# Attention scores kept in their banks: later key tiles add products with differences of neighbouring keys

## The chip, the core and the metric

The kernel runs on one core of a Trainium2 chip. The core has five engines that run at the same time and wait for each other through semaphores: TensorE (PE in the profile; PEld is its loading of weights), VectorE (DVE), ScalarE (ACT), GpSimd (POOL) and SyncE (SP), which issues most of the DMAs. Matrix products land in PSUM, in banks of 512 float32 columns per partition; DVE and ACT can read PSUM, POOL works on SBUF alone. The metric is the device time of one execution in microseconds (us).

## What is computed

The block of the reference is a gated transformer block over `x` of 8 x 1024 x 512, with a context of 8 x 1024 x 384. All of it is float32:

```
x = x + tanh(g1) * cross_attention(layernorm(x), ctx)        # 8 heads of 64
x = x + tanh(g2) * ffn(layernorm(x))                         # 16 heads of 32

cross_attention: q = x Wq, k = ctx Wk, v = ctx Wv; softmax(q k^T / 8) v; then Wo, bo
ffn:  q, k, v = x W^T + b
      q = (q / |q| + query_embedding) * softplus(temperature)
      h = softmax(q k^T / sqrt(32)) v
      out = (h * sum of gates) Wp^T + bp      # gates: top 3 of 15 routed heads and a shared one
```

What the change touches is the middle of both attentions: the scores `q k^T` less the row maximum, which the exponential is taken of.

## The kernel before

The batch is taken element by element (8 of them). Each has four chunks of kind 1 (cross attention, two heads of 64 in 128 partitions) and four of kind 2 (the second attention, four heads of 32). A chunk of either kind does the following.

- **Projections.** `project` computes `q` and `k` of the chunk, transposed: 128 rows (heads by width) x 1024 positions, in two halves of 512. Kind 2 also normalises q (`project_q`, `norms`, `scaled_q`): ACT writes `qq`, POOL squares it into `rn` (L367), PE sums the squares by head (`pn`), ACT takes logarithm and exponential (L391, L392), POOL multiplies (L393), ACT scales (L400).
- **Maxima.** POOL makes bfloat16 copies `kb` and `qb` (L409). PE multiplies them (`pm`, L424) and DVE takes the maximum over the keys (L465, or L448 with two banks at a time). The 16 or 32 rows of negated maxima go through a transpose (`pr`) and four small DMAs (L480) into the rows of `sh`: for every query of every head, minus a maximum of its scores.
- **Scores.** `attention` goes through steps (h, s): h is the half of the queries (512 of them), s the key tile. A step of kind 1 has two key tiles of 128 for two heads, so there are 4 steps in a half; a step of kind 2 has one key tile for four heads, so 8. In `score` two tiles of two banks each are taken from the pool `ps_sc`, which has exactly two such tiles, and each of the four banks gets two products: a one-row product of `ones_b` with a row of `sh`, which puts minus the maximum into every key's row (`m == 0`, `start=True`), and then the product of 128 keys with 512 queries (`m == 1`). ACT takes the exponential of each tile (L522) into `e`. In kind 2 each half of a step (tile 0 or 1) is written in turn, and which half comes first is switched when a pair of maxima products stood just before (`taken`), so that it begins with partitions that those did not use.
- **Values and sums.** `value` multiplies `e` with `v` into `av` (L609). POOL adds pairs of `e` tiles (L527), DVE adds some of these to a running one (L540), and the remaining ones are summed over the keys on PE with `ones` (`summed`, L560). ACT turns the sum into its inverse (L584, L585) and POOL multiplies (L596).

The order of the work on PE, ACT, DVE and POOL is written out by the program itself: the schedule is manual, and instructions stand in each engine's queue in the order in which the Python code emits them. A small planner keeps modelled clocks (`at["PE"]`, `at["DVE"]`, `at["POOL"]`). Constants such as `SC` (the cost of a step's scores) move these clocks, and they decide when a filler (a projection or an output product), a pair of maxima products, or a deferred action from the lists `soon` and `later` is emitted; `add` leaves a sum of exponentials to DVE only when its modelled clock is near PE's, and otherwise hands one more tile to the sums on PE. Between the two attentions `between` computes the output of kind 1, the second layernorm, and the first projections of kind 2; there, `project_q` of the second chunk first empties the list `soon`, which holds the first chunk's `scaled_q`, its copy into `kb` and `begin_maxima`, with the copy into `qb`.

Tiles come from pools by name: `k` has three buffers, `rn` one, the exponentials nine, the general PSUM tiles three.

Of the kernel before, what the change touches and what calls it, by code (L numbers as in the profile page):

```python
# [10 lines left out]
F32 = mybir.dt.float32  # L11
BF16 = mybir.dt.bfloat16
AF = mybir.ActivationFunctionType
ALU = mybir.AluOpType
AX = mybir.AxisListType

P = 128
# [4 lines left out]
def tile_gated_block(  # L22
# [38 lines left out]
    nc = tc.nc  # L61
# [5 lines left out]
    H = 512  # L67
# [13 lines left out]
    work = ctx.enter_context(tc.tile_pool(name="work", bufs=2))  # L81
# [3 lines left out]
    ps_sc = ctx.enter_context(tc.tile_pool(name="ps_sc", bufs=2, space=bass.MemoryType.PSUM))  # L85
# [120 lines left out]
    def norm(xt, key):  # L206

        mv = small.tile([P, 2], F32, tag="mv", name=f"mv_{key}", bufs=2)
        rs = small.tile([P, 1], F32, tag="rs", name=f"rs_{key}", bufs=2)
        xn = work.tile([P, D], F32, tag="wa", name=f"xn_{key}", bufs=4)  # L210
        stats(mv, xt, key)
        inverse(rs, mv)
        scaled(xn, xt, mv)
        return xn
# [41 lines left out]
    at = {"PE": 0.0, "DVE": 0.0, "POOL": 0.0}  # L256
# [10 lines left out]
    def pe(ns):  # L267
        at["PE"] += ns
# [4 lines left out]
    def pool(ns):  # L273
        at["POOL"] = max(at["POOL"], at["PE"]) + ns
# [21 lines left out]
    class Chunk:  # L296


        def __init__(self, kind, b, c):
            self.kind, self.b, self.c = kind, b, c  # L300
            self.key = f"{kind}_{b}_{c}"
            self.width = HD1 if kind == 1 else HD2
            self.nh = P // self.width
            self.nk = 4 // self.nh
            self.ns = NT // self.nk
            self.mx, self.done, self.free, self.waiting = None, 0, 0.0, False

            self.ends = (kind, b, c) == (2, B - 1, ND - 1)
            self.SC = 2200 if kind == 1 else 1250
            self.steps = [(h, s) for h in range(NH) for s in range(self.ns)]  # L310

        def loads(self, what="kq"):
# [18 lines left out]
        def project(self, st):  # L331

            begun = self.waiting
            if not begun:
                self.placed()
            halves = range(NH)
            if self.kind == 1:
                for h in halves:
                    yield from self.project_k(st, h)
                soon.append((at["PE"] + 3000, self.copied, self.kb, self.k))  # L340
                for h in halves:
                    yield from self.project_q(st, h)
            else:
                for h in halves:
                    yield from self.project_q(st, h)
                    if h or not begun:
                        yield from self.project_k(st, h)
                    yield from self.norms(h)
                soon.append((at["PE"] + 1000, self.copied, self.kb, self.k))
            soon.append((at["PE"] + 3000, self.begin_maxima))  # L350

        def project_q(self, st, h):
# [55 lines left out]
        def copied(self, out, src):  # L408
            nc.gpsimd.tensor_copy(out, src)  # L409
            pool(1050)  # L410

        def begin_maxima(self):
            self.copied(self.qb, self.q)
            self.waiting = False
            self.mx, self.done, self.free = self.maxima(), 0, at["POOL"] + 1500
# [73 lines left out]
        def score(self, step):  # L489

            h, s = step
            nh, width, key = self.nh, self.width, self.key
            order = (1, 0) if taken[0] and self.kind == 2 else (0, 1)
            taken[0] = False
            pss = {
                u: ps_sc.tile([P, 2, H], F32, tag="sc", name=f"sc_{key}_{h}_{s}_{u}") for u in order
            }

            def products(m, u):
                for j in (2 * u, 2 * u + 1):
                    kk, i = divmod(j, nh)
                    r, kc = i * width, s * self.nk + kk
                    if m == 0:
                        r += kk * HD2
                        lhsT, rhs = ones_b[r : r + 1, :], self.sh[r : r + 1, ts(h, H)]
                    else:
                        rows = slice(r, r + width)
                        lhsT, rhs = self.k[rows, ts(kc, P)], self.q[rows, ts(h, H)]  # L510
                    nc.tensor.matmul(pss[u][:, j % 2, :], lhsT=lhsT, rhs=rhs, start=(m == 0), stop=(m == 1))  # L511


            for half in [order] if self.kind == 1 else [order[:1], order[1:]]:
                for m in range(2):
                    for u in half:
                        products(m, u)
            pe(self.SC)
            e = {}
            for u in order:  # L520
                e[u] = epool.tile([P, 2, H], F32, tag="e", name=f"e_{key}_{h}_{s}_{u}")
                nc.scalar.activation(e[u], pss[u], AF.Exp)  # L522
            self.e[step] = e
# [141 lines left out]
    later, soon = [], []  # L665
# [430 lines left out]
    for t in range(NT):  # L1096
        was, xn = xn, norm(st.x[t], f"1_0_{t}")
# [91 lines left out]
```

## Time and profile before

| what | value |
|---|---|
| runs | 4901.2, 4903.87 and 4914.34 us; median 4903.87 |
| profiled execution | span 4892.8 us, from its first to its last instruction |
| around the span | the median of the runs lies 11.1 us above it; the profiled execution's own device time isn't listed apart |
| clock granted to TensorE | 0.991 of full speed on average |
| PE, DVE, ACT, POOL busy | 97%, 63%, 46%, 52% of the span |
| one element of the batch | about 605 us: 210 of kind 1, 128 between, 267 of kind 2 |

How to read the lines that follow: a group has the source line, the engine, the operation, what it writes and reads by the program's names, the shape, how often, then busy time and the mean ns of one, then how long the engine stood idle before these instructions and who ended that. In a timeline each line is a run of equal instructions: start, length, engine, line, operation, count. PE records are modelled at their ends and overlap, so what an instruction costs in a dense stretch is the distance from its start to the next start. An fp32 product has two records on PE and a bfloat16 product one.

### The profile page before, as it was taken

Reading aid. Unit: us, or ns where it says so; the run is one execution under the profiler, and the core shown is the slowest. Engines: PE = TensorE matmul, PEld = TensorE weight load, DVE = VectorE, ACT = ScalarE, POOL = GpSimd, SP = SyncE. Lnnn points to the kernel's source line nnn. Section 1 sums busy time; section 2 is a strip of 40 time slices with the busy share of each in tenths; the row PEclk is TensorE's granted clock in tenths of the full one; section 3 lists DMA queues with packets and bytes.
Section 4 is the critical chain, followed back from the end, with each engine's and each line's share of the span. In section 5 each row is a group of like instructions: output and inputs, shape, how many; then the busy total and the mean of one; then the engine's idle time right before and its main releaser. Section 6 shows DMA issues by size and latency. Waiting matters only on the chain.

```text
span 4892.8 us, 83962 instructions
## 1 busy us (share of the span) xinstructions
PE 4741.9 (97%) x35196; PEld 1428.3 (29%) x35196; DVE 3104.2 (63%) x4225; ACT 2254.3 (46%) x2916; POOL 2566.8 (52%) x1346
## 2 busy tenths in 40 slices
PE   9999999999999999999999999999999999999998
PEld 2222232222322223222232222322223222232232
DVE  4557665576656765567655576556765567655674
ACT  3435634355343553435534365343552436524364
POOL 1636646366363663636636366363663636626474
PEclk9999999999999999999999999999999999999999
DMA  2020010200103001030010300202002020010100
GB/s 81 27 97 20 26 50 27 97 22 24 50 27 102 17 24 50 27 106 14 24 57 24 102 14 24 65 23 95 14 24 68 27 88 15 16 53 25 38 1 18
DMA packets 212682, 208.11 MB, mean 43 GB/s; under 512 B 24144, under 2 KB 147024, under 8 KB 212304
## 3 DMA queue, kind: packets, MB, share of 16 engines
q1 hardware_dynamic: 212016, 202.76, 13.0%
q8 instruction: 275, 4.51, 0.4%
q14 instruction: 103, 0.84, 0.1%
q10 hardware_dynamic: 288, 0.00, 0.0%
HBM read 153.93 MB, written 48.23 MB: 41 GB/s over the span
## 4 chain that ended last, share of the span: by engine, by line
PE 78%; DVE 12%; POOL 3%; issue 3%; ACT 2%; DMA 1%; SPq 1%; ACTq 0%; DVEq 0%; POOLq 0%
PE sc L511 20%; PE av L609 17%; PE po L282 9%; PE pq L282 8%; PE pm L424 7%; PE pk L282 7%; PE pv L282 5%; DVE mx L448 4%; DVE mx L465 4%; PE sum L560 4%; DVE e L540 3%; POOL e L527 2%; ACT e L522 1%; PE pn L282 1%; SPq L480 1%
## 5 line engine op out<-in xcount | busy, mean ns | idle before, releaser
L527 POOL TENSOR_TENSOR e<-e,e 128x1024 f32<-128x1024 f32 x764 | 1858.8, 2448 | 1127.2 <-PE av L609 640.9
L522 ACT ACTIVATE e<-sc 128x1024 f32<-128x1024 f32 x1536 | 1492.6, 1021 | 1228.4 <-PE sc L511 1194.1
L465 DVE TENSOR_REDUCE mx<-pm 128x1 f32<-128x512 f32 x2332 | 1485.7, 684 | 751.9 <-PE pm L424 707.7
L511 PE MATMUL sc<-q,k 32*128 32x512 f32 (+1 forms) x6144 | 1197.8, 607 | 0.0
L609 PE MATMUL av<-e,v 128*32 128x512 f32 (+1 forms) x6144 | 1082.8, 614 | 0.0
L540 DVE TENSOR_TENSOR e<-e,e 128x1024 f32<-128x1024 f32 x427 | 803.8, 1893 | 347.6 <-POOL e L527 346.6
L424 PE MATMUL pm<-kb,qb 32*128 32x512 bf16 (+1 forms) x3072 | 630.7, 384 | 61.4 <-DVE mx L465 29.8
L448 DVE TENSOR_REDUCE mx<-pm 128x2 f32<-128x1024 f32 x370 | 427.7, 1218 | 264.8 <-PE pm L424 264.8
L511 PEld LDWEIGHTS sc<-q,k 32*128 32x128 f32 (+1 forms) x6144 | 479.3, 190 | 205.4 <-issue 192.1
L511 PE MATMUL sc<-sh,ones_b 1*128 1x512 bf16 x3072 | 412.6, 386 | 32.2 <-ACT e L522 16.1
L424 PEld LDWEIGHTS <-qb 32*128 32x128 bf16 (+1 forms) x3072 | 153.2, 92 | 931.6 <-issue 921.6
L609 PEld LDWEIGHTS av<-e,v 128*32 128x32 f32 (+1 forms) x6144 | 194.4, 118 | 617.3 <-issue 600.8
L282 PE MATMUL pq<-y1T,wq 128*32 128x512 f32 (+1 forms) x1568 | 249.6, 600 | 6.5 <-ACT r L584 2.6
L282 PE MATMUL pq<-y2T,wq 128*32 128x512 f32 x2048 | 248.6, 606 | 2.8 <-ACT rn L391 2.8
L282 PE MATMUL pk<-y2T,wk 128*32 128x512 f32 x2048 | 243.3, 595 | 0.0
L282 PE MATMUL pv<-wv,y2T 128*32 128x512 f32 x2048 | 242.8, 597 | 0.0
L282 PE MATMUL po<-wp,h2T 128*64 128x512 f32 (+1 forms) x1152 | 231.1, 596 | 0.0
L282 PE MATMUL po<-wo,h1T 128*32 128x512 f32 x2048 | 223.1, 593 | 0.0
L511 PEld LDWEIGHTS <-ones_b 1*128 1x128 bf16 x3072 | 103.3, 91 | 385.0 <-issue 360.9
L560 PE MATMUL sum<-e,ones 128*32 128x512 f32 (+1 forms) x1380 | 209.8, 595 | 0.2 <-POOL e L527 0.2
L282 PE MATMUL pk<-ctx,wk 128*32 128x512 f32 (+1 forms) x1176 | 188.7, 603 | 19.5 <-DMA ctx<-in_ctx 5.9
L393 POOL TENSOR_TENSOR qq<-qq,rn 128x512 f32<-128x512 f32 x64 | 89.6, 1400 | 207.6 <-ACT rn L392 200.0
(110 smaller groups left out, 2777.6 us busy)
## 6 DMA issues: line engine op xcount, KB each, us to landing
y<-xn SPq DMA_DIRECT2D x120, 256.0 KB
xb<-y SPq DMA_DIRECT2D x480, 64.0 KB
x<-in_x SPq DMA_DIRECT2D x64, 256.0 KB
out<-x SPq DMA_DIRECT2D x64, 256.0 KB
xs<-in_x SPq DMA_DIRECT2D x56, 256.0 KB
xn<-in_x SPq DMA_DIRECT2D x56, 256.0 KB
ctx<-in_ctx SPq DMA_DIRECT2D x7, 1536.0 KB
wq<-in_L_xattn_Wq SPq DMA_DIRECT2D x32, 256.0 KB
```

Source lines behind the costliest of these rows:

```text
L282: nc.tensor.matmul(ps[ts(j, w), :], lhsT=lhsT[:, ts(j, w)], rhs=rhs, start=start, stop=stop)
L393: nc.gpsimd.tensor_tensor(self.qq, self.qq, rn, ALU.mult)
L424: nc.tensor.matmul(ps, lhsT=self.qb[ts(i, width), ts(c, P)], rhs=self.kb[ts(i, width), ts(kh, H)], start=True, stop=True,)
L448: nc.vector.tensor_reduce(out, tiles[u], AX.X, ALU.max)
L465: nc.vector.tensor_reduce(mx[:, i * NT + c, kh : kh + 1], ps, AX.X, ALU.max)
L480: nc.sync.dma_start(out=self.sh[r : r + 1, :].rearrange("o (c q) -> o c q", c=NT), in_=rows[ts(r // width, NT), :],)
L511: nc.tensor.matmul(pss[u][:, j % 2, :], lhsT=lhsT, rhs=rhs, start=(m == 0), stop=(m == 1))
L522: nc.scalar.activation(e[u], pss[u], AF.Exp)
L527: nc.gpsimd.tensor_tensor(one, one, two, ALU.add)
L540: nc.vector.tensor_tensor(accs[-1], accs[-1], a, ALU.add)
L560: nc.tensor.matmul(ps[ts(2 * u + j, self.width), :], lhsT=ones[:, 0 : self.width], rhs=acc[n][:, j, :], start=(n == 0), stop=(n == len(acc ...
L609: nc.tensor.matmul(self.av[ts(i, width), :], lhsT=st.v[:, kc, ts(self.c * self.nh + i, width)], rhs=e[j // 2][:, j % 2, :], start=(kc == 0 ...
```

## The change

The two score tiles are taken once per half of the queries, at its first step, and kept for all its steps. The one-row products with `sh` are made at the first step only. Their sum with the first key tile's product stays in the banks, and every later step adds, without `start`, the product of the queries with the difference between this key tile and the one before in the same bank. ACT reads the banks after each step, as before.

For this the keys are turned into differences in place, after their bfloat16 copy is made: `differences` runs once per chunk. ACT copies the odd steps' keys into `was` (a buffer of the tag `rn`), POOL subtracts the even steps' keys from the odd ones, and then the copied odd ones from the even ones that follow. With w the columns of a step, these are 512 columns for the copy and the first subtraction and 256 (kind 1) or 384 (kind 2) for the second. It is put into `soon` behind the copy into `kb`, before `begin_maxima` with the copy into `qb`. The planner's cost of a step's scores is lowered from 2200 to 1950 ns and from 1250 to 1050 ns, and POOL's modelled clock is moved by 2500 ns for the differences.

Since a tile belongs to half u for a whole half of the queries, the switch of the order in kind 2 no longer decides which buffer is written first: before, the half that came first got the buffer next in turn.

```diff
-            self.SC = 2200 if kind == 1 else 1250
+            self.SC = 1950 if kind == 1 else 1050
...
                 soon.append((at["PE"] + 3000, self.copied, self.kb, self.k))
+                soon.append((at["PE"] + 3000, self.differences))
...
                 soon.append((at["PE"] + 1000, self.copied, self.kb, self.k))
+                soon.append((at["PE"] + 1000, self.differences))
             soon.append((at["PE"] + 3000, self.begin_maxima))
...
+        def differences(self):
+
+            w, n = self.nk * P, self.ns // 2
+            even, odd = (
+                self.k.rearrange("p (s o w) -> p o s w", o=2, w=w)[:, o] for o in range(2)
+            )
+            was = work.tile([P, n, w], F32, tag="rn", name=f"was_{self.key}", bufs=1)
+            nc.scalar.copy(was, odd)
+            nc.gpsimd.tensor_tensor(odd, odd, even, ALU.subtract)
+            nc.gpsimd.tensor_tensor(
+                even[:, 1:n], even[:, 1:n], was[:, 0 : n - 1], ALU.subtract
+            )
+            pool(2500)
...
-            pss = {
-                u: ps_sc.tile([P, 2, H], F32, tag="sc", name=f"sc_{key}_{h}_{s}_{u}") for u in order
-            }
+            if s == 0:
+                self.pss = {
+                    u: ps_sc.tile([P, 2, H], F32, tag="sc", name=f"sc_{key}_{h}_{u}") for u in order
+                }
+            pss = self.pss
...
-                    nc.tensor.matmul(pss[u][:, j % 2, :], lhsT=lhsT, rhs=rhs, start=(m == 0), stop=(m == 1))
+                    nc.tensor.matmul(pss[u][:, j % 2, :], lhsT=lhsT, rhs=rhs, start=(m == 0), stop=(m == 1), skip_group_check=True)
...
-                for m in range(2):
+                for m in range(1 if s else 0, 2):
```

## The prediction

> **What bounds the kernel now.** I read the page first: busy time by engine, then the chain of work that ended last.
>
> ```profile
> PE 4741.9 (97%) x35196; PEld 1428.3 (29%) x35196; DVE 3104.2 (63%) x4225; ACT 2254.3 (46%) x2916; POOL 2566.8 (52%) x1346
> ...
> PE 78%; DVE 12%; POOL 3%; issue 3%; ACT 2%; DMA 1%; SPq 1%; ACTq 0%; DVEq 0%; POOLq 0%
> ```
>
> TensorE (PE) has work 97% of the time and carries 78% of the chain. One fifth of the chain runs over other engines, so the stages have to be looked at apart. Busy time by stage of batch 3: FFN-type attention, cross attention, and the stretch between the two (columns: stretch; time; PE, weight loads, DVE, ACT, POOL busy; clock; DMA share; GB/s):
>
> ```profile
> 1595.80:1862.30 266.50, 257.31 (x2160) 77.52 (x2158) 197.61 (x244) 155.96 (x185) 179.09 (x82) 0.99 0.06 18
> 1862.30:2072.00 209.70, 208.12 (x1119) 65.41 (x1119) 116.66 (x195) 79.42 (x102) 100.00 (x51) 1.00 0.14 43
> 2072.00:2200.40 128.40, 123.03 (x1078) 34.33 (x1074) 75.93 (x90) 45.02 (x76) 43.30 (x36) 1.00 0.31 101
> ```
>
> Kind 1 (second row) is PE and nothing else. Kind 2 (first row) has PE at 97% with DVE at 74% and POOL at 67%: there other engines can be last. Next the groups that the change touches, different shapes apart:
>
> ```profile
> L522 ACT ACTIVATE e<-sc 128x1024 f32<-128x1024 f32 x1536 | 1492.6, 1021 | 1228.4 <-PE sc L511 1194.1 <-DVE e L540 29.6 <-PE pm L424 1.8
> ...
> L540 DVE TENSOR_TENSOR e<-e,e 128x1024 f32<-128x1024 f32 x427 | 803.8, 1893 | 347.6 <-POOL e L527 346.6
> ...
> L511 PE MATMUL sc<-sh,ones_b 1*128 1x512 bf16 x3072 | 412.6, 386 | 32.2 <-ACT e L522 16.1 <-DMA sh<-rows 12.0
> ```
>
> The last line is what goes. Its busy time overlaps neighbours, so the price is read as start to next start. A kind 1 step, PE's timeline (start, us, what, count):
>
> ```profile
> 1936.83 0.39 PE L511 MATMUL sc<-sh,ones_b 1*128 1x512 bf16 x4
> 1937.16 1.99 PE L511 MATMUL sc<-q,k 64*128 64x512 f32 x8
> 1938.98 0.38 PE L424 MATMUL pm<-kb,qb 64*128 64x512 bf16 x2
> ```
>
> Four one-row products hold the products back by 0.33 us. Two kind 2 steps (an fp32 product is two records):
>
> ```profile
> 1844.91 0.41 PE L511 MATMUL sc<-sh,ones_b 1*128 1x512 bf16 x4
> 1845.14 1.04 PE L511 MATMUL sc<-q,k 32*128 32x512 f32 x8
> 1846.11 1.06 PE L609 MATMUL av<-e,v 128*32 128x512 f32 x8
> 1847.28 0.39 PE L511 MATMUL sc<-sh,ones_b 1*128 1x512 bf16 x2
> 1847.50 1.04 PE L511 MATMUL sc<-q,k 32*128 32x512 f32 x4
> 1848.20 0.39 PE L511 MATMUL sc<-sh,ones_b 1*128 1x512 bf16 x2
> 1848.41 1.04 PE L511 MATMUL sc<-q,k 32*128 32x512 f32 x4
> ```
>
> In the first all four run side by side and cost 0.23 us. In the second, little lies between the scores, and each half waits until ACT has read its bank pair: the exponentials end at 1847.20 and 1848.15. Last, POOL in the stretch between, where PE stands idle until 1522.01:
>
> ```profile
> 1517.70 1.28 POOL L393 TENSOR_TENSOR qq<-qq,rn 128x512 f32<-128x512 f32 x1 [3.82 <-ACT rn L392]
> 1518.93 1.04 POOL L409 CAST kb<-k 128x1024 bf16<-128x1024 f32 x1
> 1519.91 1.04 POOL L409 CAST qb<-q 128x1024 bf16<-128x1024 f32 x1
> 1520.91 1.04 POOL L367 TENSOR_TENSOR rn<-qq 128x512 f32<-128x512 f32 x1
> ```
>
> **The change, part by part.** The sum is made against this execution's span, 4892.8 us. The median of the runs, 4903.9, lies 11.1 above it, and I add that at the end.
>
> *One-row products removed.* 256 steps of kind 1 and 512 of kind 2; the first of 4 or of 8 keeps its four. So 192 steps save 0.33 us and 448 save 0.23: 63.4 + 103.0 = 166.4 us. Kind 1 should keep its part whole. In the second kind 2 step above the products of a half could start at 1847.28 and 1848.20 instead, so a step paced by ACT gains too, as long as ACT (2.04 us per step) isn't full.
>
> *Weights no longer hidden.* A later step's first product now follows another kind of matmul directly, and its weights take 0.19 us against 0.09 for the one-row kind. Bounds: 0 to 640 x 0.10 = 64 us; a gain is excluded, since these weights are the longer ones. Nearest row: in kind 1 the same weights are loaded after the one-row products, and 0.33 less the 0.22 that a one-row product streams (1847.28 to 1847.50) leaves 0.11; after the maxima's product (1938.98) the next start comes 0.31 later, 0.09 over. So 0.02 x 640 = 13 us.
>
> *Kind 2 where PE isn't last.* In the chain of the first stretch above, DVE, POOL, ACT, SP and issue hold 30%. Of 103 us that would lose up to 30; the lower end is 0, since most of those pieces are short round trips with PE at work beside them. I take 15.
>
> *What the order does with it.* The schedule of the changed kernel has 24 fewer DVE sums of exponentials and 48 more PE products in the row sums. Four of those share 0.86 us (the sums in the chain): +10.3 us on PE. DVE is relieved of 24 x 1.89 = 45 us, for which I count nothing.
>
> *Differences in the stretch between.* ACT copies 512 columns (0.63, as ACT's L392 here), and POOL subtracts 512 and then 384 (1.28 for 512 at L393, 0.96 by size). They stand between the two casts. POOL's first cast ends at 1519.91. ACT is free after its scaling of q at 1519.83, so the copy ends near 1520.5, the subtractions near 1522.7; the second cast and the square for the next chunk come 2.8 us later, and PE's norm product, behind which everything on PE waits, too. Eight batches: 22.4 us. Bounds 8 x 2.2 = 18 (copy hidden) to 8 x 3.5 = 28 (both waits).
>
> *Differences elsewhere.* 56 other chunks. In all POOL gets 32 x (1.28 + 0.64) + 32 x (1.28 + 0.96) = 133 us and ACT 64 x 0.63 = 40. POOL idles 48% of the span and ACT 54%; that is the cover. Behind POOL's subtractions queue the adds that free exponential tiles, for which ACT already waits 29.6 us through DVE's L540. Bounds 0 to another 30 us; I take 8.
>
> *A pair of banks that stays put.* Before, each step took the pair free longest. Now pair u stays pair u, and a kind 2 step that begins with the other half than the step before must wait for the exponential that ends last. In the built order that is 172 of 448 later steps. From a score's end to that exponential's end are 2.2 us (1846.0 to 1848.15); where the PE work listed between is shorter, the missing time adds up to 46 us. The other halves wait as long in the present order, only later in the step, so the lower end is 0. I take 12.
>
> *A rule against the row.* DVE's L540 takes 1.20 us at its shortest and 1.89 on average, and it runs beside POOL. The Trainium skill, GPSIMD Engine Reference, section Key points, says that POOL shares its SBUF interfaces with VectorE and that instructions with two SBUF inputs contend. By it 133 us more of POOL, at DVE's 16% share of L540 (804 of 4893 us), would stretch DVE by about 133 x 0.16 x 0.69 / 1.89 = 8 us, an estimate; the sum by the row alone leaves this out, and with it would be 8 us later at most.
>
> Sum: 166.4 - 13 - 15 - 10.3 - 22.4 - 12 - 8 = 85.7 us. Span 4807, time 4818 us. Best end of all terms: 166.4 - 10.3 - 18 = 138, time 4766. Worst: 166.4 - 64 - 30 - 10.3 - 28 - 46 - 30 = -42, time 4946.
>
> **Rivals.**
>
> *ACT and DVE take over kind 2.* Kind 1 keeps its 63, kind 2 gives almost nothing after sums and the stretch between: 63.4 + 25 - 10.3 - 22.4 - 13 = 43, time 4861, and up to 4905 with flips and queues. For it: steps like 1847.28. Against: PE is 97% busy there and ACT only 59%.
>
> *Nothing is taken back.* 138 us or a little more, since DVE is relieved: 4740 to 4770. Against: the idle PE at 1522.01, which can only grow.
>
> *Slower, by the fixed pairs.* If each of the 172 turned steps lost a whole exponential, 1.02 us, that is 175 us and more than everything gained: 166.4 - 10.3 - 22.4 - 175 = -41, time 4945. It decides from 134 / 172 = 0.78 us per turned step. For it: ACT then stands idle while PE computes, so one late step delays the next. Against: only where under 2.2 us of PE work lie between do they wait at all, and chunk 2 of a batch turns 15 times in 128 steps.
>
> **How the numbers follow.** Forecast 0.56, own range 4770 to 4865. Takeover 0.20 (4861 to 4905), of which 0.14 still faster by over 0.3%. Nothing taken back 0.12. Slower by the fixed pairs 0.12. About 0.3%, 15 us, is what a measurement of this kernel can tell from no change. So faster 0.82, same 0.06, slower 0.12. The range 4750 to 4905 leaves out about 0.06 below and 0.14 above.
>
> **What the profile after would show.** 512 one-row products, some 36 us by the rows above instead of 202. Kind 1's last chunk, eight steps, 2 us shorter each batch. PE idle before the norm product 5.2 us instead of 2.4. ACT as releaser of the score products: 16 us before, 30 to 60 after; several hundred would be the third rival. A kind 2 chunk of 66 us should become 63. What would make me wrong is above all a wait that grows with every turned step, or products whose weights cost the full 0.10.

## The result, and the profile after

The changed kernel takes 4988.9 us (median of four runs, 4988.3 to 4990.0), the kernel before 4902.5 in the same comparison (4894.9 to 4914.3). The ratio is 1.0176, 95% interval 1.0161 to 1.019: slower by 86 us, where 86 us of gain were forecast. The profiled execution's span is 4987.1 us against 4892.8, and the mean granted clock 0.978 against 0.991.

The page after, busy time by engine and the shares of the chain:

```profile
PE 4694.9 (94%) x32732; PEld 1343.1 (27%) x32732; DVE 3096.9 (62%) x4234; ACT 2285.9 (46%) x2981; POOL 2732.9 (55%) x1474
...
PE 75%; DVE 13%; POOL 6%; ACT 3%; issue 2%; DMA 1%; SPq 0%; DVEq 0%; POOLq 0%; ACTq 0%
```

PE has 2464 instructions and 47 us of busy time less, and yet the span grew by 94 us. So PE stands idle for 141 us more than before. POOL's share of the chain doubled.

The same three stretches of an element as in the prediction, kind 2, kind 1 and the stretch between (columns: stretch; time; PE, weight loads, DVE, ACT, POOL busy; clock; DMA share; GB/s):

```profile
1613.80:1900.20 286.40, 263.40 (x1960) 70.38 (x1960) 198.58 (x249) 159.57 (x190) 191.22 (x90) 0.97 0.06 17
1900.20:2099.90 199.70, 197.05 (x1021) 62.54 (x1019) 119.66 (x195) 79.50 (x103) 104.83 (x56) 1.00 0.14 46
2099.90:2231.60 131.70, 123.01 (x1065) 34.17 (x1061) 71.33 (x86) 45.06 (x78) 47.76 (x40) 0.97 0.31 98
```

Kind 1 became 10.0 us shorter, the stretch between 3.3 longer, and kind 2 19.9 us longer, though PE has 200 instructions less to do there. The clock, 0.99 and 1.00 before in the first and third row, is 0.97.

The groups that the change touches, shapes apart (count, busy time, mean ns of one, idle time before them and its releasers):

```profile
L540 ACT ACTIVATE e<-sc 128x1024 f32<-128x1024 f32 x1536 | 1495.2, 1021 | 1238.3 <-PE sc L529 1129.1 <-DVE e L558 78.3 <-POOL e L545 29.2
L422 POOL TENSOR_TENSOR k<-k 128x512 f32<-128x512 f32 x64 | 94.2, 1472 | 122.5 <-ACT was L421 120.5
L529 PE MATMUL sc<-sh,ones_b 1*128 1x512 bf16 x512 | 83.7, 402 | 65.1 <-ACT e L540 45.7 <-DMA sh<-rows 18.7
```

The one-row products went from 3072 to 512, as the change says. ACT waits 78.3 us for DVE's adds and 29.2 for POOL's, which free exponential tiles; before it was 29.6 for DVE's.

To see which stage pays in which kernel, the table adds up a stage over the eight elements: from the first exponential of a chunk to the first exponential of the next, in the profiled execution of each kernel. The 85 to 89 us ahead of the first exponential are in the span alone. The experiments that the other columns come from follow below.

| us over 8 elements | before | s_fixed | p_pool | d_noplan | e_oldsc | after |
|---|---|---|---|---|---|---|
| kind 1, chunks 0 to 2 | 1395 | 1339 | 1341 | 1339 | 1350 | 1335 |
| kind 1, chunk 3, and between | 1278 | 1263 | 1250 | 1298 | 1285 | 1286 |
| kind 2, chunk 0 | 508 | 498 | 519 | 525 | 547 | 552 |
| kind 2, chunk 1 | 551 | 548 | 551 | 547 | 552 | 581 |
| kind 2, chunk 2 | 524 | 519 | 543 | 520 | 543 | 601 |
| kind 2, chunk 3 | 551 | 546 | 576 | 546 | 561 | 544 |
| span | 4892.8 | 4799.3 | 4866.4 | 4863.9 | 4925.8 | 4987.1 |

### The profile page after: what moved, and what is told of

Read it like the earlier page. It is cut to its first block, busy times and chain, and to the rows that moved or that the text cites. A ratio compares the mean times of both kernels' runs of the same rounds, so it can differ in the third digit from the quotient of the medians.

```text
span 4987.1 us, 79217 instructions
## 1 busy us (share of the span) xinstructions
PE 4694.9 (94%) x32732; PEld 1343.1 (27%) x32732; DVE 3096.9 (62%) x4234; ACT 2285.9 (46%) x2981; POOL 2732.9 (55%) x1474
## 4 chain that ended last, share of the span: by engine, by line
PE 75%; DVE 13%; POOL 6%; ACT 3%; issue 2%; DMA 1%; SPq 0%; DVEq 0%; POOLq 0%; ACTq 0%
PE av L627 17%; PE sc L529 17%; PE po L282 9%; PE pm L440 8%; PE pq L282 7%; PE pk L282 6%; PE pv L282 5%; DVE mx L481 5%; DVE mx L464 4%; POOL e L545 4%; PE sum L578 4%; DVE e L558 3%; PE pn L282 1%; ACT e L540 1%; POOL k L422 1%
## 5 line engine op out<-in xcount | busy, mean ns | idle before, releaser
L481 DVE TENSOR_REDUCE mx<-pm 128x1 f32<-128x512 f32 x2396 | 1525.8, 685 | 872.3 <-PE pm L440 846.7
L529 PE MATMUL sc<-q,k 32*128 32x512 f32 (+1 forms) x6144 | 1217.7, 635 | 34.8 <-ACT e L540 34.8
L558 DVE TENSOR_TENSOR e<-e,e 128x1024 f32<-128x1024 f32 x403 | 786.4, 1966 | 283.1 <-POOL e L545 281.4
L440 PE MATMUL pm<-kb,qb 32*128 32x512 bf16 (+1 forms) x3072 | 660.9, 384 | 74.3 <-DVE mx L481 41.4
L464 DVE TENSOR_REDUCE mx<-pm 128x2 f32<-128x1024 f32 x338 | 390.8, 1219 | 312.1 <-PE pm L440 312.1
L529 PEld LDWEIGHTS sc<-q,k 32*128 32x128 f32 (+1 forms) x6144 | 418.5, 189 | 459.1 <-issue 226.1
L282 PE MATMUL pk<-y2T,wk 128*32 128x512 f32 x2048 | 241.7, 594 | 0.0
L578 PE MATMUL sum<-e,ones 128*32 128x512 f32 (+1 forms) x1476 | 229.0, 598 | 3.9 <-POOL e L545 3.9
L614 POOL TENSOR_TENSOR h2T<-h2T,r 128x512 f32<-128x512 f32 x62 | 79.0, 1274 | 248.6 <-ACT r L603 244.0
L282 PE MATMUL pv<-wv,ctx 128*32 128x512 f32 x1536 | 197.2, 596 | 7.3 <-ACT v L875 7.3
```

The costliest lines, as they stand in the source:

```text
L282: nc.tensor.matmul(ps[ts(j, w), :], lhsT=lhsT[:, ts(j, w)], rhs=rhs, start=start, stop=stop)
L440: nc.tensor.matmul(ps, lhsT=self.qb[ts(i, width), ts(c, P)], rhs=self.kb[ts(i, width), ts(kh, H)], start=True, stop=True,)
L464: nc.vector.tensor_reduce(out, tiles[u], AX.X, ALU.max)
L481: nc.vector.tensor_reduce(mx[:, i * NT + c, kh : kh + 1], ps, AX.X, ALU.max)
L558: nc.vector.tensor_tensor(accs[-1], accs[-1], a, ALU.add)
L578: nc.tensor.matmul(ps[ts(2 * u + j, self.width), :], lhsT=ones[:, 0 : self.width], rhs=acc[n][:, j, :], start=(n == 0), stop=(n == len(acc ...
```

## The experiments

The theory at the start was that the subtractions hold up POOL's queue and so cost far more than their own time (the queue theory). Its rival was that the tiles kept per half cost it, the third rival of the prediction (the fixed-pair theory). A third candidate is the order that the planner writes with the lowered constants and the modelled POOL time.

### e_nodiff: the change without its differences

```diff
-            was = work.tile([P, n, w], F32, tag="rn", name=f"was_{self.key}", bufs=1)
-            nc.scalar.copy(was, odd)
-            nc.gpsimd.tensor_tensor(odd, odd, even, ALU.subtract)
-            nc.gpsimd.tensor_tensor(
-                even[:, 1:n], even[:, 1:n], was[:, 0 : n - 1], ALU.subtract
-            )
...
-                    nc.tensor.matmul(pss[u][:, j % 2, :], lhsT=lhsT, rhs=rhs, start=(m == 0), stop=(m == 1), skip_group_check=True)
+                    nc.tensor.matmul(pss[u][:, j % 2, :], lhsT=lhsT, rhs=rhs, start=(m == 0 or s > 0), stop=(m == 1), skip_group_check=True)
...
-                nc.scalar.activation(e[u], pss[u], AF.Exp)
+                nc.scalar.activation(e[u], pss[u], AF.Exp, scale=0.2)
```

> The changed kernel without the copy and the two subtractions; every engine's other work keeps its order. What is computed is not the reference's: key tiles after the first are multiplied as they are, start a new sum in their banks, and the exponent is scaled by 0.2 to stay finite. Queue theory (the subtractions hold up POOL between its two casts, POOL's adds come late, DVE's sum frees the exponential tiles late, ACT and then PE wait, and PE's clock is halved after it): the 6 us wait once per batch element and most of the 5 us wait before the norm product go, with their half-clock windows, so about 8 x (6.1 + 3.4 + 2.8 + 1.7) = 112 us less than 4989, near 4877 us. Fixed-pair theory (turned kind 2 steps wait for the exponential that ends last): those waits stay, and the time falls by the 22 us of the stretch between alone, to about 4965 us.

Measured: 4923.6 us, ratio to before 1.0044 [1.0029, 1.0059]. That lies between the two forecasts, 4877 and 4965. PE's instructions stand in the same order as in the changed kernel, so the three instructions per chunk cost 65 us. But with them gone, and 2560 one-row products gone as well, the kernel is still no faster than before. Something else takes back everything that the rows give.

### e_order01: the two tiles always in the same order

```diff
-            order = (1, 0) if taken[0] and self.kind == 2 else (0, 1)
+            order = (0, 1)
```

> The changed kernel with the order of the halves fixed to (0, 1), so that no step is turned; the rest is the same, the waits of the queue too. Fixed-pair theory: kind 2 chunks 0 and 3, where score products wait for ACT, win back 60 to 100 us, to about 4890 to 4930 us. Queue theory: the 6 us waits stay, and what the fixed order wins is about what it loses by products that begin on partitions that the maxima's products have just used; 4970 to 5010 us.

Measured: 4980.0 us, 1.016 [1.0144, 1.0177]. No step turns any more, and 9 us come back, with intervals that overlap those of the changed kernel. The third rival, which needed 134 us from the turned steps, falls; `s_fixed` below says the same.

### s_rows and s_fixed: the rows alone, and the kept tiles alone

`s_rows` is the kernel before with the one-row products at the first key tile only; its tiles rotate as before, and its order on every engine is that of before. `s_fixed` also keeps the tiles per half.

```diff
-                    nc.tensor.matmul(pss[u][:, j % 2, :], lhsT=lhsT, rhs=rhs, start=(m == 0), stop=(m == 1))
+                    nc.tensor.matmul(pss[u][:, j % 2, :], lhsT=lhsT, rhs=rhs, start=(m == 0 or s > 0), stop=(m == 1), skip_group_check=True)
...
-                for m in range(2):
+                for m in range(1 if s else 0, 2):
...
-                nc.scalar.activation(e[u], pss[u], AF.Exp)
+                nc.scalar.activation(e[u], pss[u], AF.Exp, scale=0.2)
```

In `s_fixed` in addition:

```diff
-            pss = {
-                u: ps_sc.tile([P, 2, H], F32, tag="sc", name=f"sc_{key}_{h}_{s}_{u}") for u in order
-            }
+            if s == 0:
+                self.pss = {
+                    u: ps_sc.tile([P, 2, H], F32, tag="sc", name=f"sc_{key}_{h}_{u}") for u in order
+                }
+            pss = self.pss
```

> The kernel before without the one-row products after the first key tile, and nothing else: same order on every engine, score tiles still taken in turn at each step. Not the reference's result: later key tiles carry no maximum, and the exponent is scaled by 0.2 to stay finite. If the one-row products cost what the prediction read, 0.33 and 0.23 us per step: 4902 - 166 = 4736 us. If in kind 2 they ran beside the maxima's products, as the step lengths of the changed kernel suggest (1.25 to 1.09 us with no maxima beside, 2.01 to 1.94 with them on both sides): about 72 + 50 us less, 4780 us.

> As the run with the one-row products left out, with the score tiles kept for all steps of a half of the queries as in the changed kernel; no differences, the planner's constants and the order as before. Fixed-pair theory: turned steps cost 46 to 175 us against that run. Otherwise within 15 us of it.

Measured: `s_rows` 4815.6 us, 0.9818 [0.9801, 0.9834]; `s_fixed` 4803.9 us, 0.98 [0.9785, 0.9815]; before 4904.2. So the rows alone give 89 us, neither the 166 of the prediction nor the 122 of the second forecast. Keeping the tiles costs nothing: if it does anything, it helps.

The table shows where the 89 to 100 us lie: in `s_fixed` kind 1 with the stretch between gives 71 us, and kind 2 only 23 of the 103 that were counted. Kind 1 holds what its example promised. The same surroundings as in the prediction's kind 1 step (an output product before, the maxima's product behind), PE's timeline of `s_fixed`:

```profile
1895.87 1.99 PE L513 MATMUL sc<-q,k 64*128 64x512 f32 x8
1897.69 0.38 PE L424 MATMUL pm<-kb,qb 64*128 64x512 bf16 x2
```

From start to start 1.82 us, where it took 2.15 with the rows (1936.83 to 1938.98 before): 0.33 us less. Not so kind 2. These are the same two steps as those the prediction showed from 1844.91 on, in `s_rows`:

```profile
1810.79 1.14 PE L511 MATMUL sc<-q,k 32*128 32x512 f32 x8
1811.86 1.07 PE L609 MATMUL av<-e,v 128*32 128x512 f32 x8
1813.04 2.04 PE L511 MATMUL sc<-q,k 32*128 32x512 f32 x8
1815.02 1.06 PE L609 MATMUL av<-e,v 128*32 128x512 f32 x8
```

The first step is 1.07 us up to the values' product (before 1845.14 - 1844.91 + 0.97 = 1.20), so 0.13 went and not 0.23. The second, paced by ACT, is 1.98 instead of 2.10 (1847.28 to the values at 1849.38 before). And about half of all kind 2 steps stand between maxima products, where less still is to be had. One such step of the kernel before:

```profile
2207.28 0.39 PE L424 MATMUL pm<-kb,qb 32*128 32x512 bf16 x2
2207.28 0.60 PE L511 MATMUL sc<-sh,ones_b 1*128 1x512 bf16 x4
2207.51 1.23 PE L511 MATMUL sc<-q,k 32*128 32x512 f32 x8
2208.44 0.37 PE L424 MATMUL pm<-kb,qb 32*128 32x512 bf16 x1
2209.04 0.37 PE L424 MATMUL pm<-kb,qb 32*128 32x512 bf16 x1 [0.23 <-DVE mx L465]
2209.34 1.07 PE L609 MATMUL av<-e,v 128*32 128x512 f32 x8
```

and a step of `e_nodiff` with the same neighbours, without rows:

```profile
2208.75 0.39 PE L434 MATMUL pm<-kb,qb 32*128 32x512 bf16 x2
2208.75 1.24 PE L523 MATMUL sc<-q,k 32*128 32x512 f32 x8
2209.91 0.37 PE L434 MATMUL pm<-kb,qb 32*128 32x512 bf16 x1
2210.51 0.37 PE L434 MATMUL pm<-kb,qb 32*128 32x512 bf16 x1 [0.23 <-DVE mx L475]
2210.81 1.07 PE L621 MATMUL av<-e,v 128*32 128x512 f32 x8
```

Both take 2.06 us from the first maxima product to the values. In the first, the one-row products start in the same instant as the maxima products (2207.28): they run beside them on other partitions and are nearly free. The last maxima product waits 0.23 us for DVE in both, so DVE has a part in the step's end; but already the one before it starts 1.16 us after the first in both. Over all later kind 2 steps with maxima products on both sides the median of this distance is 2.01 us before and 1.92 in `s_rows` (the mean is 1.86 in both); over those with none it is 1.20 and 1.07. Taken by kinds of step, these medians add up to about 51 us; that only 23 arrived says that other engines take the rest, which no run here shows by itself.

### e_kind1 and k1_oldplan: only kind 1 changed

```diff
-            self.SC = 1950 if kind == 1 else 1050
+            self.SC = 1950 if kind == 1 else 1250
...
                 soon.append((at["PE"] + 1000, self.copied, self.kb, self.k))
-                soon.append((at["PE"] + 1000, self.differences))
...
-            if s == 0:
+            if s == 0 or self.kind != 1:
...
-                for m in range(1 if s else 0, 2):
+                for m in range(1 if s and self.kind == 1 else 0, 2):
```

`k1_oldplan` is the same with 2200 and 1250, and without the line `pool(2500)`.

> Differences and one-row products at the first key tile only in kind 1; kind 2 as in the kernel before, with its planner constant of 1250. Both theories place the loss in kind 2 and in the stretch between, so kind 1 should give what its stages showed after the change, 2.6 + 3.1 + 1.7 + 1.9 = 9.3 us per batch element: 4903 - 74 = 4829 us. If it gives under half of that, the cost of the differences in kind 1 or the planner's order is at fault instead.

> Differences in kind 1 alone, with the planner's constants of the kernel before (2200 and 1250 ns, no time on POOL's modelled clock for the differences), so that the order is that of before but for the left out and the added instructions. If kind 1's gain is that of PE's work alone, it is the same as with the lowered constant, 4831 us within 10. If the lowered constant and POOL's time in the plan earned part of it: 4840 to 4870 us.

Measured: `e_kind1` 4831.1 us, 0.9856 [0.9841, 0.9871]; `k1_oldplan` 4847.6 us, 0.9885 [0.9869, 0.9901]. The first is as forecast (4829). Kind 1 earns most of its part with either plan. With the lowered constant and the modelled POOL time the median is 16 us lower; the intervals just touch and some runs overlap, so these aren't shown to be good by themselves, but they cost nothing here. `e_kind1` is faster than both kernels.

### b_diff: the differences alone, in the kernel before

```diff
+                soon.append((at["PE"] + 3000, self.differences))
...
+                soon.append((at["PE"] + 1000, self.differences))
...
+        def differences(self):
...
+            nc.scalar.copy(was, odd)
+            nc.gpsimd.tensor_tensor(was, odd, even, ALU.subtract)
+            nc.gpsimd.tensor_tensor(
+                was[:, 0 : n - 1], even[:, 1:n], was[:, 0 : n - 1], ALU.subtract
+            )
+            pool(2500)
```

> The kernel before, with all its one-row products, and the copy and two subtractions added at the changed kernel's places but written into the spare tile alone; the result is the reference's. Queue theory: they cost here what they cost after the change, since POOL's queue is the same: 4903 + 100 = about 5000 us, with a wait of 4 us or more for an exponential tile in kind 2. Fixed-pair theory: only the stretch between grows, 22 to 35 us, 4925 to 4940 us.

Measured: 4983.0 us, 1.0165 [1.0138, 1.0192]: 82 us for work that POOL and ACT have room for by their shares, and for the order that comes with it. That is nearer to the queue theory (5000) than to its rival (4925 to 4940), but the run can't tell the work from the order.

### e_oldsc: the change with the planner's old constants

```diff
-            self.SC = 1950 if kind == 1 else 1050
+            self.SC = 2200 if kind == 1 else 1250
```

> The changed kernel with the planner's cost of a score step back at 2200 and 1250 ns; everything else as changed. Planner theory: the lower constants draw the maxima of the last chunk to the end of kind 2's third chunk, where PE waits 7 us for them in each batch element and then runs at half clock; with the old ones that wait goes, 7 x 7 + 40 = 90 us, to about 4900 us. If the order is not at fault: 4975 to 5000 us.

Measured: 4923.9 us, 1.0041 [1.0026, 1.0056]. That is between the two forecasts. Two numbers that only move the planner's model cost 65 us. By the table they lie in the second and third chunk of kind 2 (552 to 581, 543 to 601), less what kind 1 and the fourth chunk give back. In the third, the pauses of PE of more than 0.3 us add up to 82 us in the changed kernel over eight elements, to 30 in `e_oldsc` and to 6 in `s_fixed`. The largest is one of 6.07 us at the chunk's start, in seven of the eight elements, of which `e_oldsc` has none; its lines stand in the next section.

### d_noplan, p_pool and d_dve: the differences, their plan, their engine

Between `s_fixed` (4803.9) and `e_oldsc` (4923.9) stand the differences and the order that their 2500 ns of modelled POOL time brings. `d_noplan` has the first without the second, `p_pool` the second without the first:

```diff
-            pool(2500)
```

is the edit of `d_noplan` against `e_oldsc`. `p_pool` is `e_nodiff` with

```diff
-            self.SC = 1950 if kind == 1 else 1050
+            self.SC = 2200 if kind == 1 else 1250
```

and `d_dve` is `d_noplan` with

```diff
-            nc.gpsimd.tensor_tensor(odd, odd, even, ALU.subtract)
-            nc.gpsimd.tensor_tensor(
+            nc.vector.tensor_tensor(odd, odd, even, ALU.subtract)
+            nc.vector.tensor_tensor(
```

> The change with the planner's constants of before and without the 2500 ns by which POOL's modelled clock is moved for the differences. Its instructions stand on PE in the order of the kernel before without later one-row products and with kept banks (4803.9 us), and the copy and the two subtractions come on top. With the modelled POOL time the same work took 4923.9. Theory A (the order that the modelled time brings costs most of the 120 us between them): 4825 to 4865. Theory B (the subtractions in POOL's queue cost most of it, whatever the order): 4880 to 4925.

> The kernel that takes 4923.9 us (the change with the planner's constants of before) without the copy and the two subtractions: later key tiles begin their sums anew, and the exponential's argument is scaled by 0.2 so that it stays in range; this leaves out the maxima from the second key tile on. The modelled POOL time stays, so its order on PE is that of the kernel with 4923.9. Theory A: 4870 to 4915, most of the distance to 4803.9 stays. Theory B: 4804 to 4840.

> As the first of these three, with the two subtractions on DVE in place of POOL; DVE's work in such a chunk grows by about 2 us. If POOL's queue is what the differences cost, this is faster than the first by at least half of what the first stands above 4803.9. If the cost is that begin_maxima waits for the whole chain of copy and subtractions on any engine, it is the same or slower, since DVE is busier than POOL in kind 2.

Measured: `d_noplan` 4868.5 us, 0.9937 [0.9921, 0.9954]; `p_pool` 4868.9 us, 0.9934 [0.9919, 0.9949]; `d_dve` 5084.8 us, 1.0376 [1.036, 1.0391]. Neither theory had it: each half costs 65 us, and the two together 120.

By the table the instructions cost 35 us in the last chunk of kind 1 with the stretch between, 27 in the first chunk of kind 2, and nothing elsewhere. Both places can be read. First the stretch between, in the changed kernel, POOL and PE together:

```profile
1533.44 1.04 POOL L411 CAST kb<-k 128x1024 bf16<-128x1024 f32 x1
1535.00 1.26 POOL L422 TENSOR_TENSOR k<-k 128x512 f32<-128x512 f32 x1 [0.52 <-ACT was L421]
1536.34 0.99 POOL L423 TENSOR_TENSOR k<-k,was 128x384 f32<-128x384 f32 x1
1537.27 1.04 POOL L411 CAST qb<-q 128x1024 bf16<-128x1024 f32 x1
1538.27 1.04 POOL L369 TENSOR_TENSOR rn<-qq 128x512 f32<-128x512 f32 x1
1539.36 1.93 PE L282 MATMUL pn<-rn,hsum 128*32 128x512 f32 x8 [5.24 <-POOL rn L369]
1541.07 5.00 PE L282 MATMUL pq<-y2T,wq 128*32 128x512 f32 x32
1545.90 1.89 PE L282 MATMUL pk<-y2T,wk 128*32 128x512 f32 x16
```

The pause is the one that was forecast: 5.24 us, `d_noplan` has the same. What comes behind it was not. PE's norm product now holds its place for 1.71 us (1539.36 to 1541.07) where it took 0.88 before (1522.01 to 1522.89), and the next 32 records take 4.83 instead of 3.6 (24 took 2.69). The stretch's own row says why (the clock is the third figure from the end):

```profile
1537.00:1543.80 6.80, 4.44 (x24) 1.16 (x28) 0.00 (x0) 1.23 (x2) 3.29 (x4) 0.50 0.00 0
```

Before the change the same stretch was

```profile
1522.01 1.07 PE L282 MATMUL pn<-rn,hsum 128*32 128x512 f32 x8 [2.38 <-POOL rn L367]
1522.89 2.76 PE L282 MATMUL pq<-y2T,wq 128*32 128x512 f32 x24
```

After this pause of 2.38 us the clock stayed at full speed (1.00 from 1519.6 to 1528.4); with 5.24 us it is at half until 1543.8. That costs 0.83 + 1.2 = 2 us more in this element. The changed kernel has these 6.8 us in every element, and the kernel before has a half-clock stretch of 3.4 us at this place in three of its eight. The net cost is some 13 us over eight, on top of 23 us of longer pauses; in `d_noplan` the two sums are about the same, and its stretch between is 35 us longer.

The Trainium skill, TensorE: Matmul & The Clock Gate, section "What's actually happening", says that the clock falls to half after at least one idle window of about 3.4 us and returns after a busy one. The row fits it: half clock from within a pause of 5.24 us, for 6.8 us in all. The three stretches before the change don't, since their pauses of 2.38 us are shorter than that window; the measurement decides.

The second place is the first chunk of kind 2 in `d_noplan`. Its timeline, POOL first, then DVE and PE:

```profile
2187.52 1.27 POOL L423 TENSOR_TENSOR k<-k 128x512 f32<-128x512 f32 x1 [3.95 <-ACT was L422]
2188.86 1.00 POOL L424 TENSOR_TENSOR k<-k,was 128x384 f32<-128x384 f32 x1
2189.81 1.04 POOL L412 CAST qb<-q 128x1024 bf16<-128x1024 f32 x1
2190.80 9.33 POOL L545 TENSOR_TENSOR e<-e,e 128x1024 f32<-128x1024 f32 x4
2202.27 5.64 POOL L545 TENSOR_TENSOR e<-e,e 128x1024 f32<-128x1024 f32 x2 [2.14 <-ACT e L540]
2197.94 3.27 DVE L558 TENSOR_TENSOR e<-e,e 128x1024 f32<-128x1024 f32 x1
2201.13 1.28 DVE L481 TENSOR_REDUCE mx<-pm 128x1 f32<-128x512 f32 x2
2202.33 3.38 DVE L558 TENSOR_TENSOR e<-e,e 128x1024 f32<-128x1024 f32 x1
2205.63 2.47 DVE L481 TENSOR_REDUCE mx<-pm 128x1 f32<-128x512 f32 x4
2206.36 0.37 PE L440 MATMUL pm<-kb,qb 32*128 32x512 bf16 x1 [2.12 <-DVE mx L481]
```

POOL had waited 3.95 us for the copy; then its adds come four in a row, and two more later. DVE's two adds, one beside each of these groups, take 3.27 and 3.38 us, the maxima stand behind these in DVE's queue, and PE waits 2.12 us for them. In `s_fixed`, with the same order on PE, DVE's adds at this place are:

```profile
2168.03 2.16 DVE L542 TENSOR_TENSOR e<-e,e 128x1024 f32<-128x1024 f32 x1
2171.49 1.22 DVE L542 TENSOR_TENSOR e<-e,e 128x1024 f32<-128x1024 f32 x1
```

and PE doesn't wait. The pause of 2.1 us comes once in seven of the eight elements. Over the span, PE's pauses above 0.3 us are 23 us longer in the stretch between and 17 in this chunk; the time lost at half clock (the length of the half-clock stretches, halved) rises from 44 to 71 us. These make up the 65 us, with some overlap, since the clock is also at half during a pause.

`d_dve` shows what it means to choose the engine by its place in the queue. The two groups of the maxima products of kind 2, first `d_noplan`:

```profile
L440 PE MATMUL pm<-kb,qb 32*128 32x512 bf16 x2048 | 431.3, 382 | 77.9 <-DVE mx L481 45.0 <-DVE mx L464 23.9 <-POOL qb L412 4.0
```

and `d_dve`:

```profile
L440 PE MATMUL pm<-kb,qb 32*128 32x512 bf16 x2048 | 448.1, 394 | 195.2 <-DVE mx L481 149.8 <-DVE mx L464 39.1 <-ACT part L591 2.7
L423 DVE TENSOR_TENSOR k<-k 128x512 f32<-128x512 f32 x64 | 63.2, 988 | 289.5 <-ACT was L422 189.2 <-POOL kb L412 90.1 <-ACT e L540 10.2
```

DVE's subtractions are shorter (988 ns against 1272), but DVE stands still for 289.5 us in front of them, waiting for the copy and for the cast of the same keys, and the maxima are queued behind. The kernel loses 216 us against `d_noplan`; the second of its forecasts, the same or slower, came true.

What the order of `p_pool` costs is spread over three chunks of kind 2 (519, 543 and 576 against 498, 519 and 546), while the stretch between gains 13. Most of it can be read at one place, the end of the third chunk, where the fourth begins with its one-row products:

```profile
2372.89 0.39 PE L524 MATMUL sc<-sh,ones_b 1*128 1x512 bf16 x1 [2.66 <-DMA sh<-rows]
```

PE waits for the DMAs that bring the next chunk's maxima, in all eight elements; in `s_fixed` it does so for more than 2 us in the last element alone, and here waits 0.15 us (2349.21). Over the span the third chunk has 30 us of pauses of PE against 6, and the fourth loses 41 us at half clock against 11, most of it in stretches of 6.8 and 10.2 us that begin within 2.5 us of this pause. They match the 24 and 30 us by which the two chunks are longer. In the whole span the half-clock loss is 73 us against 44. `e_oldsc` and the changed kernel have this wait in every element too. Which of the moved entries makes the maxima late was not tried one by one.

### best: no differences in the first chunk of kind 2

If the differences cost only around the first chunk of kind 2, this chunk can stay as it was. The edit is against `d_noplan`:

```diff
-                soon.append((at["PE"] + 1000, self.differences))
+                if self.c:
+                    soon.append((at["PE"] + 1000, self.differences))
...
-                for m in range(1 if s else 0, 2):
+                for m in range(1 if s and (self.kind, self.c) != (2, 0) else 0, 2):
```

> The change with the planner's constants of before, no modelled POOL time for the differences, and the first chunk of kind 2 as before: one-row products at every key tile and no differences. Between the kernel with kept banks and no differences (4803.9 us) and the same with differences (4868.5) the stretch from kind 1's last chunk to kind 2's first lost 35 us and kind 2's first chunk 27, all other stages together about 3. If the cost of the differences sits in that one chunk's chain (its copy and subtractions stand before the second cast, the maxima and the norms), this gives 4804 + 3 + 10 (what the chunk itself gains without one-row products) = 4817, range 4805 to 4832. If the cost moves to the next chunk instead, 4845 to 4870.

Measured: 4834.4 us (4826.5 to 4843.1), 0.987 [0.9853, 0.9887]: 34 us faster than `d_noplan`, but 17 above the forecast and just outside its range. The stretch between came back whole (1260 against 1298), the first chunk mostly (514 against 525, with its one-row products again), and 13 us moved to the second (560 against 547). So the cost around this chunk is what it was taken for, but a part of it comes back in the next chunk; why is not shown. With `e_kind1` (4831.1) it can't be told apart; these two are the fastest that leave nothing of the computation out.

## Why the prediction was wrong

The account in medians, from the runs above:

| step | us | how |
|---|---|---|
| one-row products go, tiles kept | -100 | `s_fixed` less before |
| the copy and the two subtractions | +65 | `d_noplan` less `s_fixed` |
| the order from 2500 ns of modelled POOL time | +55 | `e_oldsc` less `d_noplan` |
| the order from the lowered constants | +65 | after less `e_oldsc` |
| sum | +85 | measured: 4988.9 less 4904.2 |

The terms hold in this sequence. Two of them were measured in another one as well: the 2500 ns cost 65 us without the differences (`p_pool` less `s_fixed`), and the lowered constants 55 (`e_nodiff` less `p_pool`). They don't simply add up everywhere: in the kernel with its one-row products the differences and their plan cost 82 us (`b_diff`), not 120.

- **"One-row products removed", 166.4 us: the kind 2 half failed.** Kind 1 was right (71 us by stages for 63.4). In kind 2 the price of 0.23 us was read at one step without maxima products and taken for all 448. Of that step itself 0.13 was to be had, and of a step between maxima products some 0.09, since the rows run beside those. 23 us arrived in place of 103. The takeover rival described this ("kind 2 gives almost nothing"), but for another reason in part, and got 0.20.
- **"Weights no longer hidden", 13 us.** In kind 1 nothing of it is seen (0.33 of 0.33 kept). In kind 2 the shown step lost 0.10 of 0.23, the upper bound of this term. By itself it was not measured.
- **"What the order does with it", 10.3 us: the step that failed worst.** Only the row sums and the turned steps were counted in the new order; that the planner's clocks also shift when maxima, adds and scalings are emitted was given no term and no upper bound. It costs 55 + 65 us. The first comes largely with the wait for late maxima and the half clock behind it, the second with the pauses of the third chunk (30 to 82 us). Both changes to the model are visible in the diff. The worst end of all terms, 4946, could not reach the result for this reason above all.
- **"Differences in the stretch between", 22.4 us.** The pause is as forecast to the tenth: 2.38 to 5.24 us, 23 us in all by the traces. The term was still too small, 35 us by stages, since the half clock with such a pause was left out.
- **"Differences elsewhere", 8 us.** The cover was taken from POOL's idle share of the span. About 30 us by `d_noplan`, nearly all in one chunk of eight: there POOL's adds bunch up, and DVE's adds and maxima behind them are late. In the changed kernel's own order there is one more place, in seven of eight elements, here POOL, then DVE, ACT and PE:

```profile
2358.54 2.04 POOL L411 CAST kb<-k 128x1024 bf16<-128x1024 f32 x1
2360.66 2.13 POOL L422 TENSOR_TENSOR k<-k 128x512 f32<-128x512 f32 x1
2367.18 3.35 DVE L558 TENSOR_TENSOR e<-e,e 128x1024 f32<-128x1024 f32 x1 [5.52 <-POOL e L545]
2370.62 1.94 ACT L540 ACTIVATE e<-sc 128x1024 f32<-128x1024 f32 x2 [6.39 <-DVE e L558]
2371.70 0.61 PE L529 MATMUL sc<-sh,ones_b 1*128 1x512 bf16 x2 [6.07 <-ACT e L540]
```

  The cast takes 2.04 us for 1.04, the subtraction 2.13 for 1.26, the adds queue behind them, no exponential tile is free, and PE stands for 6.07 us, with the clock at half when it goes on. The order has the larger part in it: without the differences (`e_nodiff`) PE still stands for 3.80 us here, and with them in the old constants' order (`e_oldsc`) no such pause occurs. The prediction had named this queue and both groups, and priced it from an average.
- **"A pair of banks that stays put", 12 us, and the third rival.** Too high: nothing, by `s_fixed` and `e_order01`. The sign given for the rival, ACT as the releaser of score products for several hundred us, was wrong as well. In the changed kernel the score line's wait for ACT is 280.2 us, but in `s_fixed`, 100 us faster than before, it is 241.7. Before it was 16.1. Some 200 of the 280 us are idle time of the weight loads (by shape 160.0 and 39.7), which run beside the matmuls; that is no idle time of PE. What is left for the products is 80 us, against 48 in `s_fixed`.
- **The rule of the Trainium skill on POOL and DVE** (GPSIMD Engine Reference, section Key points) would have made it 8 us later at most. DVE's 427 adds take 839.3 us in `d_noplan` and 826.4 in `s_fixed`, 13 us more; but in `s_rows`, which has no subtractions either, they take 835.4, so no run here shows a part of it that is due to the subtractions. What a longer add costs depends on what is queued behind it.
- Of what the profile was to show, 512 one-row products, kind 1's last chunk 1.9 us shorter per element (259.5 to 243.9 us over eight, from its first exponential to the end of its last) and the 5.2 us before the norm product came true. A kind 2 chunk of 66 us did not become 63: the first went from 63.5 to 69.

## What to carry to other kernels

An instruction's price, read start to start at one example, holds only for steps with the same neighbours: where it runs beside other matmuls on other partitions it is nearly free, so group the steps by what stands around them before multiplying. A change that also moves a planner's constants is two changes: run the order apart from the work, since here each of the two planner edits cost about as much as the work did. And a few us of work in an engine with half its time idle must be priced by what is queued behind it at each place, with the half clock that comes with a pause of PE added.

## What the runs showed of the hardware

- In the changed kernel a pause of PE of 5.2 to 6.1 us comes with 6.8 us at half clock in element after element (at 1537.0 and 1752.1 us, 2154.9 and 2369.9; once 10.2), partly within the pause. In `d_noplan` three of the eight pauses of 5.2 us come with 3.4 us only. The length of a pause alone doesn't decide: three of the eight pauses of 2.4 us in the kernel before came with 3.4 us at half clock and five with none, and the waits of 2.05 to 2.67 us for the maxima rows at the end of the third chunk came with 6.8 or 10.2 us each time, in `p_pool` and in the changed kernel (there 0.3 us behind a pause of 1.63). The time lost at half clock is 42 us in the kernel before, 109 in the changed one and 175 in `d_dve`.
- One-row products of 1 partition and maxima products of 32 start in the same instant (2207.28) here, where they use other partitions.
- POOL's copies and subtractions have a spread of two at the same shape: the cast 1.04 to 2.04 us, the subtraction of 512 columns 1.26 to 2.13, where DVE works beside them (its adds ran from 2356.72 to 2361.66); DVE's add of two tiles 1.22 to 3.38.
